# An output projection by seven products of half-size blocks, in two attention layers of a fused network

## The chip, the core and the metric

The kernel runs on one core of a Trainium2 chip. The metric is the device time of one execution in microseconds; the median of three executions is given, and a profile of one execution shows where the time lies. The core's engines are named TensorE (PE), VectorE (DVE), ScalarE (ACT), GpSimd (POOL) and SyncE (SP); SyncE issues the transfers spoken of here.

## The reference

Four layers work on x of shape 2 x 512 x 32 x 32 (batches, channels, pixels). Layer 0 is a deformable attention with an MLP, layer 1 a linear attention. Layers 2 and 3, the ones that matter, are both a self-attention with eight heads of 64 channels over 1024 pixels; they differ in the number of groups of the normalisation:

```python
xn  = group_norm(x)                                  # 8 groups in layer 2, 32 in layer 3
qkv = einsum('oc,bcn->bon', qkv_w, xn) + qkv_b       # 1536 x 512 weights
q, k, v = heads of qkv
attn = softmax(einsum('bhcn,bhcm->bhnm', q, k) * 64 ** -0.5)
att  = einsum('bhnm,bhcm->bhcn', attn, v)            # 512 channels x 1024 pixels
x    = x + einsum('oc,bcn->bon', proj_w, att) + proj_b
```

The last line is the output projection: a 512 x 512 weight times a 512 x 1024 matrix, for each of two batches. All is computed in float32.

## The kernel before

x stays in SBUF the whole time, as `xs[b][t]`: per batch four tiles of 128 channels by 1024 pixels. `P` is 128, `CT` = 4 the tiles of channels, `HF` = 512 half of the pixels, `DH` = 64, `NB` = 8 blocks of 128 keys.

Layers 2 and 3 go through `attention`, which first makes queries, keys and values (`queries_keys_values`) and then, where a bound on the logits holds (it does for these inputs), runs `heads_bounded`. The other branch, `heads_general`, is built but not executed.

Queries, keys and values are already made by seven products in place of eight. A matrix product of 2 x 2 blocks can be had from seven products of sums of the blocks, in Winograd's form of Strassen's scheme. The table `SEVEN` (line 50) says for P1 to P7 which of seven left operands (the four blocks of the weight and three sums, `left_sums`, L624) meets which of seven right operands. The MLP of layer 0 does the same (L649 its matmuls, L628 to L631 the sums of its weights, L763, L764 and L767 adds to x on GpSimd).

`heads_bounded` has 16 units: batch b, pair of heads p, half of the pixels h. A unit has 8 steps, one per block of 128 keys. In a step TensorE computes scores (L1246, 4 matmuls) into a PSUM tile of the ring `ps_s` (two tiles), ScalarE takes the exponential into an SBUF tile tagged `e` (L1250, pool `ep` of six), and TensorE multiplies it with the values two steps later (L1275). The sum of the exponentials over the keys is shared: GpSimd adds e0+e1, then e3 and e5 (L1255, L1257, tile `some`), VectorE adds e2+e4, e6, e7 and then `some` (L1260, L1262, L1264). L1284 and L1285 add two halves of a unit's output into the tile of its query (`data[b][0][p]`, named q in the profile). `divide`, four steps into the next unit, sums the exponentials over partitions on TensorE (L1292), copies (L1296), adds (L1297), takes the reciprocal (L1298), multiplies (L1300) and adds the bias of the values (L1301).

After the last unit the projection runs: for each batch and each of four tiles of 128 output channels `project_block` issues 8 matmuls (two halves of the pixels by four tiles of input channels) into one tile of `ps_s`, and VectorE evicts the two halves with bias and residual in one instruction each (L607). The last unit's `divide` stands behind the first block. In layer 2 the statistics of layer 3's normalisation for batch 0 (`channel_means`, L1171 and L1172; `group_means`, L1178 to L1189; `norm_first`) are issued behind blocks 1 to 6; in layer 3 each half is stored to the output as soon as it is evicted (L609). The projection's weights are loaded at the start of `heads_bounded` (L947, four transfers of 256 KB per layer).

TensorE's order is the order of the code (`manual_schedule`); the order on the other engines in `heads_bounded` is decided by a scheduler, which also gives free buffers of a tag to the next tile that asks. [...] Where two engines touch the same PSUM bank, the framework puts them one after the other.

Of the kernel before, what the change touches and what calls it, by code (L numbers as in the profile page):

```python
# [11 lines left out]
F32 = mybir.dt.float32  # L12
AF = mybir.ActivationFunctionType
ALU = mybir.AluOpType
# [4 lines left out]
P = 128  # L19
B, C, H, W = 2, 512, 32, 32  # L20
N = H * W
CT = C // P
NB = N // P
HF = 512
# [25 lines left out]
SEVEN = {"P1": (0, 0), "P2": (1, 2), "P3": (6, 3), "P4": (3, 6), "P5": (2, 4), "P6": (4, 5), "P7": (5, 1)}  # L50


class Net:
# [539 lines left out]
    def project_block(self, acc, att, w, bias: str, b: int, o: int, out):  # L593

        nc = self.nc
        for h in range(2):
            for t in range(CT):
                nc.tensor.matmul(  # L598
                    acc[:, h, :],
                    lhsT=w[t][:, o * P : (o + 1) * P],  # L600
                    rhs=att[t][:, h * HF : (h + 1) * HF],
                    start=(t == 0),
                    stop=(t == CT - 1),
                )
        for h in range(2):
            xt = self.xs[b][o][:, h * HF : (h + 1) * HF]
            nc.vector.scalar_tensor_tensor(xt, acc[:, h, :], self.col(bias, o), xt, ALU.add, ALU.add)  # L607
            if out is not None:
                nc.sync.dma_start(out[b, o][:, h * HF : (h + 1) * HF], xt)  # L609
# [330 lines left out]
            self.nc.sync.dma_start(got[-1], src)  # L940
        return got

    def projection_weights(self, pool, k: int):
        got = []
        for t in range(CT):
            got.append(pool.tile([P, C], F32, tag=f"proj{t}", name=f"proj{k}{t}"))
            self.nc.sync.dma_start(got[-1], self.io[f"l{k}_proj"][t])  # L947
        return got

    def averages(self):  # L950
        self.avg, self.means = {}, {}
        for k in (2, 3):
            self.avg[k] = self.norm.tile([P, P], F32, tag="avg", name=f"avg{k}")
            self.nc.sync.dma_start(self.avg[k], self.io[f"l{k}_avg"])

    def attention(self, k: int, weights, out, meanwhile=lambda: None):


        nc = self.nc
        with ExitStack() as ctx:  # L960
            one = self.pool(ctx, f"a{k}")
            ones = one.tile([P, DH], F32, tag="ones", name=f"ones{k}")
            nc.vector.memset(ones, 1.0)
            data = []
            for b in range(B):
                qs = [one.tile([P, N], F32, tag=f"q{b}{t}", name=f"q{k}{b}{t}") for t in range(CT)]
                ks = [one.tile([P, N], F32, tag=f"k{b}{t}", name=f"k{k}{b}{t}") for t in range(CT)]
                v = [one.tile([P, 2, C], F32, tag=f"v{b}{n}", name=f"v{k}{b}{n}") for n in range(NB // 2)]
                data.append((qs, ks, v))
            small_logits, got = self.queries_keys_values(k, weights, ones, data, meanwhile)  # L970
            if k == 2:
                self.means_tiles(3, 0)
                self.first[3] = self.first_block(3, 0)

            with self.tc.If(small_logits > 0) as cmp:
                self.heads_bounded(k, ones, data, out)
            with cmp.Else():
                self.heads_general(k, data)
                with ExitStack() as ctx2:
                    proj = self.projection_weights(self.pool(ctx2, f"a{k}_w_p"), k)  # L980
                    ps = self.pool(ctx2, f"a{k}_ps_p", 2, psum=True)
                    for b in range(B):
                        for o in range(CT):
                            acc = ps.tile([P, 2, HF], F32, tag="ps", name=f"pbg{k}{b}{o}")
                            self.project_block(acc, data[b][0], proj, f"pb{k}", b, o, out)
                    if k == 2:
                        for t in range(CT):
                            self.channel_means(3, 0, t)
                        for _ in self.group_means(3, 0, ps.tile([P, 2, HF], F32, tag="ps", name="gm3g")):
                            pass  # L990
                        self.norm_first(3)
            return got
# [227 lines left out]
    def heads_bounded(self, k, ones, data, out):  # L1220
# [5 lines left out]
        nc = self.nc  # L1226
        halves = [slice(0, DH), slice(DH, P)]
        with ExitStack() as ctx:
            proj = self.projection_weights(self.pool(ctx, f"b{k}_w"), k)
            ep = self.pool(ctx, f"b{k}_e", 6)  # L1230
            ap = self.pool(ctx, f"b{k}_a", 1)
            ap2 = self.pool(ctx, f"b{k}_a2", 2)
            ps_s = self.pool(ctx, f"b{k}_ps_s", 2, psum=True)
            ps_o = self.pool(ctx, f"b{k}_ps_o", 1, psum=True)
# [52 lines left out]
            def divide(unit):  # L1287
                b, p, h, state = unit
                d = ps_o.tile([P, 2, HF], F32, tag="d", name=f"d{k}{b}{p}{h}")
                for r, rows in enumerate(halves):  # L1290
                    for par in range(2):
                        nc.tensor.matmul(  # L1292
                            d[halves[par], r, :], lhsT=ones[rows, :], rhs=state["sum"][rows, par, :], start=True, stop=True
                        )
                t = ap.tile([P, HF], F32, tag="r", name=f"r{k}{b}{p}{h}")
                nc.scalar.copy(t, d[:, 0, :])  # L1296
                nc.vector.tensor_tensor(t, d[:, 1, :], t, ALU.add)  # L1297
                nc.vector.reciprocal(t, t)  # L1298
                res = data[b][0][p][:, h * HF : (h + 1) * HF]
                nc.vector.tensor_tensor(res, res, t, ALU.mult)  # L1300
                nc.vector.tensor_scalar(res, res, self.col(f"vb{k}", p), None, ALU.add)  # L1301

            units = [(b, p, h, {}) for b in range(B) for p in range(CT) for h in range(2)]
            steps = [(unit, n) for unit in units for n in range(NB)]
            with self.tc.manual_schedule(engines={mybir.EngineType.PE}):


                for i in range(len(steps) + 5):
                    if i < len(steps):
                        score(*steps[i])  # L1310
                    for j in ([], [i - 3, i - 2])[i % NB == 3] if i % NB in (2, 3) else [i - 2]:
                        if 0 <= j < len(steps):
                            value(*steps[j])
                    if i % NB == 4 and NB < i < len(steps):
                        divide(steps[i - NB][0])
                for b in range(B):
                    for o in range(CT):
                        acc = ps_s.tile([P, 2, HF], F32, tag="s", name=f"pb{k}{b}{o}")
                        self.project_block(acc, data[b][0], proj, f"pb{k}", b, o, out)
                        if b == o == 0:  # L1320
                            divide(units[-1])
                        if k == 2:
                            n = b * CT + o
                            if 1 <= n <= CT:
                                self.channel_means(3, 0, n - 1)
                            elif n == CT + 1:
                                steps = self.group_means(3, 0, ps_o.tile([P, 2, HF], F32, tag="d", name="gm3"))
                                next(steps)
                            elif n == CT + 2:
                                next(steps, None)  # L1330
                                self.norm_first(3)

    def heads_general(self, k, data):
        with ExitStack() as ctx:
# [102 lines left out]
def _blocks(w):  # L1437

    return np.ascontiguousarray(w.T).reshape(-1, P, w.shape[0])


def _slabs(w):


    s0, _, s1, m = w.shape
    w = w.reshape(s0, 2, 2, P, s1, 2, m // 2).transpose(0, 4, 3, 5, 1, 2, 6)
    return w.reshape(s0 * s1, P, 4, 2, m // 2)
# [30 lines left out]
def _layout(i):  # L1478
    f = {k: np.asarray(v) for k, v in i.items()}
    a = {k[8:]: v for k, v in f.items() if k.startswith("L0_conv_")}  # L1480
    l1 = {k[8:]: v for k, v in f.items() if k.startswith("L1_conv_")}
    l2 = {k[8:]: v for k, v in f.items() if k.startswith("L2_conv_")}
    l3 = {k[8:]: v for k, v in f.items() if k.startswith("L3_conv_")}
# [5 lines left out]
    def over(v):  # L1489
# [33 lines left out]
        "l1_b": np.concatenate([l1["bv"], l1["bq"], l1["bk"]]),  # L1523
        "l2_qk": _slabs(l2["qkv_w"][: 2 * C].T.reshape(1, C, 1, 2 * C))[0],
        "l2_v": _slabs(l2["qkv_w"][2 * C :].T.reshape(1, C, 1, C))[0],
        "l2_proj": _blocks(l2["proj_w"]),
        "l2_avg": _average(C // 8),
        "l3_qk": _slabs(w3[: 2 * C].T.reshape(1, C, 1, 2 * C))[0],
        "l3_v": _slabs(w3[2 * C :].T.reshape(1, C, 1, C))[0],
        "l3_proj": _blocks(l3["w_proj"]),  # L1530
        "l3_avg": _average(C // 32),
    }

# [15 lines left out]
```

## Time and profile before

The time before is 3453.8 us (median of 3 runs, 3453.35 to 3453.96). The profiled execution has a span of 3450.1 us, with a mean granted TensorE clock of 0.997. Busy microseconds of each engine in the stretches of layers 2 and 3, by start and end in the span:

| Stretch | us | PE | DVE | ACT | POOL |
|---|---|---|---|---|---|
| heads of layer 2, 2702.4 to 2942.7 | 240.3 | 236.3 | 164.7 | 146.3 | 113.6 |
| projection of layer 2, to 3001.1 | 58.4 | 56.9 | 27.2 | 4.0 | 9.7 |
| queries, keys, values of layer 3, to 3149.5 | 148.4 | 147.5 | 89.9 | 25.1 | 53.1 |
| heads of layer 3, to 3389.1 | 239.6 | 236.1 | 164.4 | 145.0 | 113.4 |
| projection of layer 3 and end, to 3450.1 | 61.0 | 56.4 | 20.0 | 1.2 | 0.0 |

In a row of the timeline the first number is the start in us from the beginning of the span, the second the time from there to the end of what was merged into the row; then engine, line of the code, operation, written and read tiles, shape and count. What stands in brackets is idle time of that engine just before, and what ended it. A float32 matmul shows as two records, so 64 matmuls of a projection are 128 records. PEld is the load of weights into the array and SPq the issue of a transfer by SyncE.

### The profile page before, as it was taken

What the parts mean: (1) busy time and instruction counts of PE and PEld (TensorE: products, weight loads), DVE (VectorE), ACT (ScalarE), POOL (GpSimd) and SP (SyncE); (2) the same over time, 40 slices, a digit from 0 to 9 for tenths busy, and PEclk for the clock granted to TensorE, in tenths of its full rate; (3) what the DMA queues carried; (4) which work ended last, traced back from release to release, by engine and by line L of the source; (5) the groups of instructions that cost most, each with busy time, mean ns of one, the idle gap of its engine ahead of it and who ended that gap; (6) DMA issues with size and microseconds to landing.
All of it is one profiled execution on the core that took longest, in us unless ns stands there. A gap on an engine that the chain in (4) does not pass through costs nothing.

```text
span 3450.1 us, 60119 instructions
## 1 busy us (share of the span) xinstructions
PE 3394.9 (98%) x25280; PEld 1260.6 (37%) x25280; DVE 2313.2 (67%) x2539; ACT 2017.4 (58%) x2100; POOL 2078.3 (60%) x1584
## 2 busy tenths in 40 slices
PE   7999999999999999999999999999999999999999
PEld 2333333333333333333333334444555433455333
DVE  6877777777767567777776764575556577555774
ACT  5877877887787577877887761111111466113661
POOL 4778777787787577787788874442323444234441
PEclk9999999999999999999999999999989999999999
DMA  6878777877887577887888872111000100000001
GB/s 154 156 144 159 149 155 146 156 158 141 157 161 141 108 156 149 155 157 144 167 168 158 159 152 76 49 37 37 1 1 0 50 1 2 1 0 13 2 1 50
DMA packets 103247, 342.64 MB, mean 99 GB/s; under 512 B 12720, under 2 KB 14384, under 8 KB 100144
## 3 DMA queue, kind: packets, MB, share of 16 engines
q0 software_dynamic: 73296, 266.90, 41.0%
q1 hardware_dynamic: 28656, 69.68, 6.8%
q8 instruction: 202, 3.31, 0.4%
q10 hardware_dynamic: 1008, 2.06, 0.2%
q14 instruction: 85, 0.70, 0.1%
HBM read 67.27 MB, written 4.46 MB: 21 GB/s over the span
## 4 chain that ended last, share of the span: by engine, by line
PE 80%; DVE 15%; ACT 2%; POOL 1%; issue 1%; DMA 0%; DVEq 0%; ACTq 0%; SPq 0%; POOLq 0%
PE hp L486 46%; DVE h L455 3%; PE pb L598 3%; DVE r L1298 3%; PE sim L518 3%; PE o L1275 2%; DVE sum L1262 2%; PE s L1246 2%; PE qk20P L1041 1%; PE qk30P L1041 1%; PE m_0P L649 1%; PE qk21P L1041 1%; PE m_5P L649 1%; PE m_4P L649 1%; PE m_2P L649 1%; PE qk31P L1041 1%
## 5 line engine op out<-in xcount | busy, mean ns | idle before, releaser
L486 PE MATMUL hp<-h,w 128*32 128x512 f32 x16384 | 1831.1, 593 | 5.5 <-DVE h L455 3.6
L455 DVE CUSTOM_DVE_ANT_1 h<-tx,bank 128x1024 f32<-128x1024 f32 x1024 | 1180.4, 1215 | 332.9 <-PE hp L486 310.6
L491 ACT ACTIVATE h<-hp,magb 128x1024 f32<-128x1024 f32 x1024 | 1122.0, 1111 | 416.7 <-PE hp L486 415.6
L486 PEld LDWEIGHTS hp<-h,w 128*32 128x32 f32 x16384 | 543.1, 110 | 1216.1 <-issue 1120.9
L478 POOL DMA_DIRECT2D h<-h x509 | 451.7, 1023 | 392.5 <-ACT h L497 334.0
L504 POOL TENSOR_TENSOR h<-h,h 128x1024 f32<-128x1024 f32 x255 | 613.5, 2406 | 21.3
L502 POOL TENSOR_SCALAR h<-h,flip 128x1024 f32<-128x1024 f32 x256 | 447.7, 1749 | 0.9 <-ACT h L491 0.9
L1250 ACT ACTIVATE e<-s 128x1024 f32<-128x1024 f32 x256 | 258.2, 1024 | 177.6 <-PE s L1246 164.1
L493 ACT ACTIVATE h<-h,flip 128x1024 f32<-128x1024 f32 x256 | 291.3, 1138 | 0.0
L1275 PE MATMUL o<-e,v 64*64 64x512 f32 x2048 | 261.0, 592 | 6.7 <-DVE q L1285 6.7
L1246 PE MATMUL s<-q,k 64*64 64x512 f32 x2048 | 259.8, 589 | 2.6 <-DVE v L1079 1.8
L1257 POOL TENSOR_TENSOR some<-some,e 128x1024 f32<-128x1024 f32 x64 | 151.5, 2367 | 75.7 <-ACT e L1250 73.3
L495 POOL TENSOR_SCALAR h<-h,flip 128x1024 f32<-128x1024 f32 x128 | 144.9, 1132 | 77.4 <-ACT h L491 76.0
L1255 POOL TENSOR_TENSOR some<-e,e 128x1024 f32<-128x1024 f32 x32 | 75.5, 2361 | 190.8 <-DVE sum L1264 155.6
L497 ACT ACTIVATE h<-h,flip 128x1024 f32<-128x1024 f32 x128 | 145.6, 1137 | 0.0
L518 PE MATMUL sim<-h,ends 128*32 128x512 f32 x1024 | 141.0, 592 | 0.0
L1260 DVE TENSOR_TENSOR sum<-e,e 128x1024 f32<-128x1024 f32 x32 | 46.4, 1451 | 136.1 <-ACT e L1250 136.1
L1275 PEld LDWEIGHTS o<-e,v 64*64 64x64 f32 x2048 | 75.8, 133 | 157.3 <-issue 123.7
L1246 PEld LDWEIGHTS s<-q,k 64*64 64x64 f32 x2048 | 78.7, 133 | 143.4 <-issue 117.9
L628 POOL TENSOR_TENSOR mlp_w<-mlp_w 128x512 f32<-128x512 f32 x16 | 22.4, 1401 | 161.0 <-DMA mlp_w<-in_mlp_w 136.7
L708 ACT ACTIVATE mh<-mh,cols 128x512 f32<-128x512 f32 x64 | 46.2, 722 | 124.2 <-DVE mh L726 65.5
L1029 POOL TENSOR_TENSOR sq<-q 128x512 f32<-128x512 f32 x32 | 33.3, 1039 | 139.7 <-DVE q L1048 95.6
(456 smaller groups left out, 3280.2 us busy)
## 6 DMA issues: line engine op xcount, KB each, us to landing
h<-h POOLq DMA_DIRECT2D x509, 512.0 KB, 6.5
lb<-logs SPq DMA_DIRECT2D x63, 512.0 KB, 5.2
mlp_w<-in_mlp_w SPq DMA_DIRECT2D x16, 1024.0 KB, 4.9
x<-in_x SPq DMA_DIRECT2D x8, 512.0 KB, 9.7
qkw<-in_l_qk SPq DMA_DIRECT2D x2, 2048.0 KB, 8.3
out<-x SPq DMA_DIRECT2D x16, 256.0 KB, 2.1
vw<-in_l_v SPq DMA_DIRECT2D x2, 1024.0 KB, 7.4
proj<-in_l_proj SPq DMA_DIRECT2D x8, 256.0 KB, 5.1
```

What stands on the lines that cost most here:

```text
L455: self.nc.vector._custom_dve(TENSOR_ADD_SAT, out=h[:, k, :, :], in0=x[:, jj, 2 * r + k, :].unsqueeze(1).to_broadcast([P, H, W]), in1=y[:, ...
L478: nc.gpsimd.dma_start(to, what, accum_op=ALU.add)
L486: nc.tensor.matmul(hp[rows, cut], lhsT=self.l0w2[:, 32 * q : 32 * q + 32], rhs=h1[k][:, cut], start=True, stop=True)
L491: nc.scalar.activation(y, hp, AF.Relu, bias=self.magb[:, q : q + 1])
L493: nc.scalar.activation(ys[0], ys[0], AF.Copy, scale=self.flip[:, 0:1])
L502: nc.gpsimd.tensor_scalar(y, y, self.flip[:, 2:3], 1.0, ALU.mult, ALU.mult)
L504: (nc.vector if final else nc.gpsimd).tensor_tensor(y, y, ys[2], ALU.add)
L518: nc.tensor.matmul(sims[u][at : at + 32, :], lhsT=self.ends[:, 28 - 4 * o : 60 - 4 * o], rhs=z[jj][:, h * HF : (h + 1) * HF], start=(o == ...
L1246: nc.tensor.matmul(s[halves[c], par, :], lhsT=ks[p][rows, at : at + DH], rhs=qs[p][rows, cut], start=True, stop=True)
L1250: nc.scalar.activation(e, s, AF.Exp, scale=DH**-0.5)
L1257: nc.gpsimd.tensor_tensor(state["some"], state["some"], e, ALU.add)
L1275: nc.tensor.matmul(o[halves[par], r, :], lhsT=v[n // 2][rows, n % 2, at : at + DH], rhs=e[rows, par, :], start=(n == 0), stop=(n == NB - 1),)
```

## The change

In layers 2 and 3 the projection, too, is done by seven products of halves in place of eight: the weight's 512 x 512 is cut into four blocks of 256 x 256, and the attention's 512 x 1024 into four of 256 x 512. A product is 4 matmuls (two tiles of output channels by two of input channels), and a batch takes 7 products.

It is for fewer matmuls on TensorE. In return there are sums:

- of the weights (`project_left`): four of 128 x 512 on GpSimd per layer, written in the code after step 72 of 128. The weights are one transfer of 1 MB in a layout of blocks.
- of the attention (`project_right`): eight of 128 x 512 per batch, all on GpSimd in batch 0, half of them on VectorE in batch 1. Their four tiles of 128 x 1024 are taken from the ring of the exponentials, tag `e`, which goes from six tiles to five, since the weights and their three sums need more room.
- of the products (`project`): ScalarE copies P1 into a tile `u`; VectorE adds products to x or to `u`; GpSimd adds `u` to x where more than one block of the output needs it.

The last unit's `divide` now stands behind P1 of batch 0, and the statistics of layer 3 for batch 0 behind P1, P3, P6 and P7 of batch 1, as x of batch 0 is complete only after P4.

In the order in which the changed program is built, the four weight sums come first on GpSimd in each `heads_bounded`, ahead of e0+e1 of the first unit. On VectorE the first batch reads: the last unit's sums, a sum for batch 1, L1285, evictions of P1, L1297, the reciprocal, evictions of P3 alternating with L1300 and L1301, evictions of P2.

```diff
-            proj = self.projection_weights(self.pool(ctx, f"b{k}_w"), k)
-            ep = self.pool(ctx, f"b{k}_e", 6)
+            wp = self.pool(ctx, f"b{k}_w", 1)
+            ep = self.pool(ctx, f"b{k}_e", 5)
...
+            def project_left():
+                w = wp.tile([P, 7, 2, 2 * P], F32, tag="proj", name=f"proj{k}")
+                nc.sync.dma_start(w[:, 0:4], self.io[f"l{k}_proj"])
+                self.left_sums(nc.gpsimd, w[:, 0:4], w[:, 4:7])
+                return [w[:, i] for i in range(7)]
+
+            def project_right(b):
+                att = data[b][0]
+                r = [[att[2 * (i // 2) + c][:, (i % 2) * HF : (i % 2 + 1) * HF] for c in range(2)] for i in range(4)]
+                t = [ep.tile([P, 2, HF], F32, tag="e", name=f"pt{k}{b}{i}") for i in range(4)]
+                t1, t2, t3, t4 = ([x[:, c, :] for c in range(2)] for x in t)
+                for c in range(2):
+                    eng = nc.vector if b == 1 and c == 0 else nc.gpsimd
+                    eng.tensor_tensor(t1[c], r[1][c], r[0][c], ALU.subtract)
+                    eng.tensor_tensor(t2[c], r[3][c], t1[c], ALU.subtract)
+                    eng.tensor_tensor(t3[c], r[3][c], r[1][c], ALU.subtract)
+                    eng.tensor_tensor(t4[c], r[2][c], t2[c], ALU.subtract)
+                return [r[0], t3, r[2], r[3], t1, t2, t4]
...
+                for which in ("P1", "P3", "P2", "P6", "P7", "P5", "P4"):
+                    a, ri = SEVEN[which]
...
+                    acc = ps_s.tile([P, 2, HF], F32, tag="s", name=f"pb{k}{b}{which}")
+                    for p in range(2):
+                        for c in range(2):
+                            nc.tensor.matmul(acc[:, p, :], lhsT=left[a][:, c, p * P : (p + 1) * P],
+                                             rhs=right[ri][c], start=c == 0, stop=c == 1)
+                    for p in range(2):
+                        got = acc[:, p, :]
+                        u = us[:, p, :]
+                        if which == "P1":
+                            nc.scalar.copy(u, got)
+                            add(vec, p, 0, got, True)
+                        elif which == "P3":
+                            add(vec, p, 1, got, True)
+                        elif which == "P2":
+                            add(vec, p, 0, got)
+                            store(p, 0)
+                        elif which == "P6":
+                            vec.tensor_tensor(u, got, u, ALU.add)
+                        elif which == "P7":
+                            u3 = u3s[:, p, :]
+                            vec.tensor_tensor(u3, got, u, ALU.add)
+                            add(pool, p, 3, u3)
+                            add(pool, p, 2, u3)
+                        elif which == "P5":
+                            vec.tensor_tensor(u, got, u, ALU.add)
+                            add(pool, p, 1, u)
+                            store(p, 1)
+                            add(vec, p, 3, got, True)
+                            store(p, 3)
+                        else:
+                            add(vec, p, 2, got, True)
+                            store(p, 2)
+                    yield
...
-                for b in range(B):
-                    for o in range(CT):
-                        acc = ps_s.tile([P, 2, HF], F32, tag="s", name=f"pb{k}{b}{o}")
-                        self.project_block(acc, data[b][0], proj, f"pb{k}", b, o, out)
-                        if b == o == 0:
-                            divide(units[-1])
...
+                    if i == len(steps) // 2 + NB:
+                        left = project_left()
+                right = project_right(0)
+                for n, _ in enumerate(project(0, left, right)):
+                    if n == 0:
+                        divide(units[-1])
+                    elif n == 1:
+                        right = project_right(1)
+                for n, _ in enumerate(project(1, left, right)):
+                    if k == 2:
+                        if n < 2:
+                            self.channel_means(3, 0, 2 * n)
+                            self.channel_means(3, 0, 2 * n + 1)
+                        elif n == 3:
+                            means = self.group_means(3, 0, ps_o.tile([P, 2, HF], F32, tag="d", name="gm3"))
+                            next(means)
+                        elif n == 4:
+                            next(means, None)
+                            self.norm_first(3)
```

The calls `add` and `store` add to the block i of x with or without the bias, and store it where the layer is the last.

## Prediction

> **What bounds the kernel now.** I read the page first: engine shares, then the chain that ended last.
>
> ```profile
> PE 3394.9 (98%) x25280; PEld 1260.6 (37%) x25280; DVE 2313.2 (67%) x2539; ACT 2017.4 (58%) x2100; POOL 2078.3 (60%) x1584
> ...
> PE 80%; DVE 15%; ACT 2%; POOL 1%; issue 1%; DMA 0%; DVEq 0%; ACTq 0%; SPq 0%; POOLq 0%
> ```
>
> TensorE is busy 98% of the span and carries the chain, so a matmul less is time gained unless TensorE waits instead. Next, the timeline of the end of layer 3's heads and the first projection blocks:
>
> ```profile
> 3386.40 2.75 PE L1275 MATMUL o<-e,v 64*64 64x512 f32 x24
> ...
> 3389.09 7.13 PE L598 MATMUL pb<-q,proj 128*128 128x512 f32 x16
> ...
> 3390.95 1.23 DVE L1264 TENSOR_TENSOR sum<-sum,some 128x1024 f32<-128x1024 f32 x1
> ...
> 3398.65 3.35 DVE L1298 RECIPROCAL r<-r 128x512 f32<-128x512 f32 x1
> ...
> 3411.21 1.41 DVE L607 SCALAR_TENSOR_TENSOR x<-pb,cols,x 128x512 f32<-128x512 f32 x2 [5.46 <-PE pb L598]
> ```
>
> A block of 8 matmuls (16 records) is 7.13 us, less the 0.27 by which a last record overhangs: 6.86, or 0.858 us a matmul. TensorE does not pause; VectorE idles 5.46 of every 6.87 us; GpSimd does nothing. This is the room that the change fills. Third, the start of the heads of layer 3, where the timeline shows what the weight sums can hold up:
>
> ```profile
> 3149.54 3.23 SPq L947 DMA_DIRECT2D proj<-in_l_proj  x4
> ...
> 3152.91 2.36 POOL L1255 TENSOR_TENSOR some<-e,e 128x1024 f32<-128x1024 f32 x1 [12.52 <-ACT e L1250]
> ...
> 3157.50 1.02 ACT L1250 ACTIVATE e<-s 128x1024 f32<-128x1024 f32 x1 [0.69 <-PE s L1246]
> ...
> 3159.81 1.07 PE L1246 MATMUL s<-q,k 64*64 64x512 f32 x8
> ```
>
> The rows are the load of the projection's weights, GpSimd's first sum (e0+e1), exponential number 5 (counted from 0) and score 7. Last, the same kind of load and sums in layer 0:
>
> ```profile
> 2185.64 0.33 SPq L672 DMA_DIRECT2D mlp_w<-in_mlp_w  x1
> 2190.63 1.27 POOL L628 TENSOR_TENSOR mlp_w<-mlp_w 128x512 f32<-128x512 f32 x1 [5.47 <-DMA mlp_w<-in_mlp_w]
> 2191.98 1.27 POOL L629 TENSOR_TENSOR mlp_w<-mlp_w 128x512 f32<-128x512 f32 x1
> ```
>
> From issue of 1 MB to the first sum: 5.0 us; then one sum each 1.345 us.
>
> [...] L1260, two SBUF inputs beside GpSimd's sums, takes 1.45 us in the mean, where L1264 takes 1.23. [...] no row of before has both read one bank. [...] here 1.27 against 0.69 us for 128x512 (L1081, L1285).
>
> **The change, part by part.**
>
> *Matmuls.* Per layer 64 become 2 x 7 x 4 = 56: 8 x 0.858 = 6.86 us less, 13.7 in both.
>
> *Weight sums.* The four sums are written after step 72, but the scheduler puts them first on GpSimd, ahead of e0+e1, in both layers. Queued behind them are all sums "some" of the first unit. With five exponential buffers, exponential 5 needs the buffer of e0 or e1, so it waits for e0+e1; score 7 needs the PSUM tile that exponential 5 reads; TensorE stands at score 7. Layer 3: load issued 3149.54, + 5.0 = 3154.54; four sums to 3159.85; e0+e1 to 3162.3 (2.36); exponential 5 to 3163.4; score 7 at 3163.4 instead of 3159.81: 3.6 us. Layer 2, where the load is issued at 2702.91 and score 7 starts at 2713.82: 2707.9, 2713.2, 2715.7, 2716.7, so 3.0 us. Sum 6.6. Later units catch up nothing, since TensorE is full.
>
> *Five buffers elsewhere.* In a steady unit (3373 to 3388) exponential 7 starts at 3386.7 and needs e2, whose last reader (L1260) ends at 3383.1; exponential 5 starts at 3383.2 and needs e0, read until 3379.6. The margins are over 3 us: nothing.
>
> *Sums of the attention for the first batch.* Eight on GpSimd, 10.2 us, beginning when its last "some" ends, 2.3 us before the projection. The first is needed by P6, 11.15 us into the projection: ready at about 2.8. Nothing.
>
> *VectorE's queue in the first batch.* P6 needs the PSUM tile of P3, whose second eviction stands behind this row, counted from the projection's start: sums until 3.1; a sum for the second batch 0.69; L1285 0.68; P1's evictions, which alternate with ScalarE's copies of the same banks (0.75, 0.58, 0.75), until 6.8; L1297 0.69; reciprocal 3.35, until 10.9; P3's first half 0.75, L1300 0.69, second half 0.75: 13.04. TensorE is ready at 11.15: 1.95 us, in each layer.
>
> *Border of the batches.* P1 of batch 1 waits for P5's evictions (four VectorE instructions of 0.69 to 0.75 behind one more sum): 0.4 us in each layer. In layer 2 the statistics of batch 0, until now spread behind blocks with 5.46 us of room each, queue up here: the eviction of P4 stands behind a statistic that waits for GpSimd's last adds to x (6 x 1.27 plus a sum after P7), which costs P3 0.86 us; the evictions of P1 stand behind six more statistics of 0.67, which costs P2 2.03.
>
> So layer 3's projection gains 6.86 - 2.35 = 4.5, layer 2's 6.86 - 5.24 = 1.6.
>
> *Contention.* Three sums for batch 1 are released on VectorE and GpSimd by the same matmul, both reading two SBUF inputs. At no cost 0; at the 1.8 and 0.95 us that such pairs show in layer 0 (L628 up to 1.79, L638 0.952), carried through the same queue, 1.7 us for both layers; at 2.25 and 1.2 (the slowest adds of L764 and L763 there) 3.4. I take 1.
>
> *End.* After P7 of batch 1 GpSimd does six adds of 1.27: it ends about 1.7 us after the last matmul, as VectorE does, but the last store of x now stands in SyncE's order behind three others that wait for those adds, about 0.35 each (L672): 1.1 us. At the border to layer 3, evictions end 0.1 later; GpSimd's query-key weight sums (four of 2.4) move from 2957 to behind its adds, ready some 11.5 us after the projection, while the first product that needs them, the third, starts at 1.55 (the gap before L1041) + 2 x 6.86 = 15.3: nothing.
>
> Sum: -13.7 + 6.6 + 2.35 + 5.24 + 1.2 + 1.0 = +2.7 us.
>
> **Rivals.** (a) *The queues are looser than I count*: reciprocal and evictions interleave so that P6 and the border cost nothing. Then -13.7 + 6.6 + 1.2 = -6, 3448. If GpSimd's late first sum also cost nothing, 3441: the gain in full. For it: VectorE is under half busy in the projection on average (27.15 of 58.40 us in layer 2). Against: its queue is in order and the row of work at the start is fixed. (b) *Slower*: the loads land after 7.4 us, as vw of the attention layers does in the page's issues (+4.8 for both), and contention takes 3.4: +10, 3464. For it: all the terms sit on TensorE. Against: the load is alone on its queue, as in layer 0.
>
> **How the numbers follow.** Forecast (losses about equal the saving, within 0.2%, 6.9 us): 0.80; rival (a), in full, faster: 0.06; rival (b), or a wait that I don't see, slower: 0.14. Predicted: 3453.8 + 2.7 = 3456.5. Low: rival (a)'s first form, 3448.5; high: contention 3.4 and loads at 6 us (+2.4 +2), 3461.5.
>
> **What would show it.** Right: score 7 of each layer's first unit 3 to 3.6 us late, released by ScalarE, GpSimd's e0+e1 behind L628 to L631; TensorE idle before P6 about 2 us with the reciprocal on VectorE; layer 2's P3 and P2 of batch 1 waiting on VectorE; the two projections near 57 and 52 us. Wrong: exponential 5 on time, or no gap in the projections (then 3441 to 3448), or a wait in each unit of the heads (then far over 3461).

## The result and the profile after

The changed kernel takes 3473.1 us in the median (3472.9 to 3474.2, 4 runs) where the kernel before takes 3453.9 (3453.4 to 3456.6): the ratio is 1.0055, with a 95% interval of 1.0037 to 1.0072. It is slower by 19 us; the prediction was 3456.5, and its range ended at 3461.5.

The page of the changed kernel, first its busy times, then the chain that ended last:

```profile
PE 3391.0 (98%) x25248; PEld 1256.5 (36%) x25248; DVE 2361.7 (68%) x2579; ACT 2022.5 (58%) x2108; POOL 2162.1 (62%) x1640
...
PE 77%; DVE 17%; ACT 2%; POOL 2%; issue 1%; DMA 1%; DVEq 0%; SPq 0%; POOLq 0%; ACTq 0%
```

TensorE has 32 matmul records fewer and 3.9 us less busy time, not the 13.7 us that 16 matmuls of 0.858 us should take away: what remains must be running slower somewhere. VectorE has gained 48 us of busy time with only 40 instructions more, which at some 0.7 us each are 28, so others have become longer; its share of the chain went from 15% to 17%. Next, what TensorE waited for in layers 2 and 3 (us in total, times, longest):

```profile
PE s L1240 <- ACT e L1244: 10.9, 3, 6.0
PE d L1286 <- DVE sum L1258: 7.8, 2, 3.9
PE pb21P L1345 <- DVE x L1326: 2.1, 3, 0.9
PE pb31P L1345 <- DVE x L1326: 0.6, 1, 0.6
PE pb20P L1345 <- DVE x L1326: 0.4, 1, 0.4
```

The first row is the wait of score 7 that was forecast, and larger (0.8 us of it stood in the kernel before too). The second was not forecast at all: `d` is the product of the last unit's divisor (L1286), and it waits for VectorE's last addition of exponentials. The waits at P6 (pb20P) and at the border of the batches (pb21P, pb31P) were forecast, and are smaller. The timeline of the start of the heads of layer 2:

```profile
2704.19 0.33 SPq L1301 DMA_DIRECT2D proj<-in_l_proj  x1
2711.79 1.27 POOL L628 TENSOR_TENSOR proj<-proj 128x512 f32<-128x512 f32 x1 [17.21 <-DMA proj<-in_l_proj]
2713.14 2.13 POOL L629 TENSOR_TENSOR proj<-proj 128x512 f32<-128x512 f32 x1
2717.91 2.34 POOL L1249 TENSOR_TENSOR some<-e,e 128x1024 f32<-128x1024 f32 x1
2720.28 1.94 ACT L1244 ACTIVATE e<-s 128x1024 f32<-128x1024 f32 x2 [8.17 <-POOL some L1249]
2721.36 1.99 PE L1240 MATMUL s<-q,k 64*64 64x512 f32 x8 [6.05 <-ACT e L1244]
```

The chain is the forecast one: the load, four sums (two are shown), e0+e1, exponential 5, score 7. But the load took 7.6 us from issue to the first sum, where 5.0 had been taken. And the last row holds a surprise: 8 records take 1.99 us, where 8 such records took 1.07 in the row shown of before. The timeline of the start of the projection of layer 2 in the changed kernel:

```profile
2952.01 3.70 PE L1345 MATMUL pb20P<-q,proj 128*128 128x512 f32 x8
2952.61 3.65 POOL L1314 TENSOR_TENSOR pt<-q,pt 128x512 f32<-128x512 f32 x2
2952.85 4.49 DVE L1256 TENSOR_TENSOR sum<-sum,e 128x1024 f32<-128x1024 f32 x2
2957.45 2.10 DVE L1258 TENSOR_TENSOR sum<-sum,some 128x1024 f32<-128x1024 f32 x1
2959.60 1.47 PE L1286 MATMUL d<-sum,ones 64*64 64x512 f32 x8 [3.88 <-DVE sum L1258]
2961.00 8.40 PE L1345 MATMUL pb20P<-q,proj 128*128 128x512 f32 x16
2969.84 2.38 PE L1345 MATMUL pb20P<-pt,proj 128*128 128x512 f32 x5 [0.44 <-DVE x L1326]
```

VectorE's two additions of e take 4.49 us, where before they took 2.55 (2941.93); the last one takes 2.10, where it took 1.23. GpSimd adds attention tiles at the same time, two in 3.65 us, where one alone takes 1.27. So the divisor's product stands for 3.88 us, and the 16 records behind it take 8.40 in place of 7.13. Last, the windows view of the first 3 us after the wait at score 7 and of the next 3. A row gives the stretch and its length, the busy us (and instructions) of PE, PEld, DVE, ACT and POOL, then the granted TensorE clock, the DMA share and GB/s:

```profile
2721.30:2724.30 3.00, 2.94 (x16) 1.05 (x20) 1.50 (x1) 1.78 (x3) 2.92 (x2) 0.50 0.01 3
2724.30:2727.30 3.00, 3.00 (x28) 0.86 (x24) 2.70 (x2) 1.18 (x2) 1.66 (x1) 0.94 0.00 0
```

After the wait TensorE gets half its clock for some 3 us. Finer windows give the bounds of all such stretches in layers 2 and 3: 2717.8 to 2724.6 (it began while TensorE still stood at score 7), 2960.2 to 2963.6, 3175.2 to 3178.6 and 3414.1 to 3417.6, each behind one of the four long waits. TensorE had work for 3.3, 3.4, 2.8 and 3.4 us of them, and half of that is lost: 1.6, 1.7, 1.4 and 1.7 us, 6.4 in all.

By stretch, before and after: the heads of layer 2 take 240.3 and 248.3 us, the projection of layer 2 58.4 and 60.9, queries, keys and values of layer 3 148.4 both times, the heads of layer 3 239.6 and 244.9, the projection of layer 3 with the end 61.0 and 64.9. That is +8.0, +2.5, 0, +5.3 and +3.9; the remaining 1.3 of the 21.0 us between the two spans lies ahead of layer 2, where nothing was changed.

Theories for the runs. **First:** the four weight sums hold up score 7. **Second:** GpSimd's additions exclude VectorE's, so that the divisor comes late. **Third:** after such a wait TensorE runs at half clock. Rivals: five buffers of exponentials cost time in every unit; VectorE's queue is late on its own; the order of TensorE's products is what matters.

### The profile page after: what moved, and what is told of

It reads as the page before. It is cut to its first block, busy times and chain, and to the rows that moved or that the text cites. A ratio compares the mean times of both kernels' runs of the same rounds, so it can differ in the third digit from the quotient of the medians.

```text
span 3471.1 us, 60176 instructions
## 1 busy us (share of the span) xinstructions
PE 3391.0 (98%) x25248; PEld 1256.5 (36%) x25248; DVE 2361.7 (68%) x2579; ACT 2022.5 (58%) x2108; POOL 2162.1 (62%) x1640
## 3 DMA queue, kind: packets, MB, share of 16 engines
q10 hardware_dynamic: 1008, 2.06, 0.2%
## 4 chain that ended last, share of the span: by engine, by line
PE 77%; DVE 17%; ACT 2%; POOL 2%; issue 1%; DMA 1%; DVEq 0%; SPq 0%; POOLq 0%; ACTq 0%
PE hp L486 46%; DVE r L1292 3%; DVE h L455 3%; PE sim L518 3%; DVE sum L1256 2%; PE o L1269 2%; PE qk20P L1035 1%; PE qk30P L1035 1%; PE m_0P L649 1%; PE m_6P L649 1%; PE m_4P L649 1%; PE m_3P L649 1%; PE m_1P L649 1%; PE qk31P L1035 1%; PE qk21P L1035 1%; PE m_5P L649 1%
## 5 line engine op out<-in xcount | busy, mean ns | idle before, releaser
L1244 ACT ACTIVATE e<-s 128x1024 f32<-128x1024 f32 x256 | 258.2, 1024 | 190.8 <-PE s L1240 176.5
L1240 PE MATMUL s<-q,k 64*64 64x512 f32 x2048 | 261.6, 593 | 12.7 <-ACT e L1244 10.9
L1269 PE MATMUL o<-e,v 64*64 64x512 f32 x2048 | 262.2, 595 | 6.4 <-DVE q L1279 6.4
L1269 PEld LDWEIGHTS o<-e,v 64*64 64x64 f32 x2048 | 75.9, 133 | 158.6 <-issue 125.4
L628 POOL TENSOR_TENSOR mlp_w<-mlp_w 128x512 f32<-128x512 f32 x16 | 22.6, 1415 | 160.6 <-DMA mlp_w<-in_mlp_w 130.7
L1292 DVE RECIPROCAL r<-r 128x512 f32<-128x512 f32 x32 | 107.3, 3353 | 1.1
```

Of the source, the lines that this page charges most:

```text
L1240: nc.tensor.matmul(s[halves[c], par, :], lhsT=ks[p][rows, at : at + DH], rhs=qs[p][rows, cut], start=True, stop=True)
L1244: nc.scalar.activation(e, s, AF.Exp, scale=DH**-0.5)
L1269: nc.tensor.matmul(o[halves[par], r, :], lhsT=v[n // 2][rows, n % 2, at : at + DH], rhs=e[rows, par, :], start=(n == 0), stop=(n == NB - 1),)
```

## Experiments on the first wait

**Five buffers alone.** The kernel before with one number changed.

```diff
-            ep = self.pool(ctx, f"b{k}_e", 6)
+            ep = self.pool(ctx, f"b{k}_e", 5)
```

> The kernel before with five buffers of the exponentials in place of six, nothing else. Theory (the weight sums on GpSimd, not the buffer count, hold up the first unit): 3454 us, no difference, no wait of score 7 in either layer, heads 240 us each. Rival (five buffers cost time by themselves, all through the heads): the 13.3 us by which the two heads grew, so about 3467.

Measured: 3454.1 us against 3453.9, ratio 1.0002 (0.9993 to 1.0010). The rival of five buffers falls; that step of the prediction ("nothing") held.

**The weight sums with eight products.** The eight products of the kernel before, with five buffers. The weights come in one load of 1 MB, and four sums are added, which go to spare tiles.

```diff
+                w = wp.tile([P, 7, 2, 2 * P], F32, tag="proj", name=f"proj{k}")
+                nc.sync.dma_start(w[:, 0:4], self.io[f"l{k}_proj"])
+                nc.gpsimd.tensor_tensor(w[:, 5], w[:, 0], w[:, 2], ALU.subtract)
+                nc.gpsimd.tensor_tensor(w[:, 4], w[:, 2], w[:, 3], ALU.add)
+                nc.gpsimd.tensor_tensor(w[:, 5], w[:, 4], w[:, 0], ALU.subtract)
+                nc.gpsimd.tensor_tensor(w[:, 6], w[:, 1], w[:, 5], ALU.subtract)
```

> The eight products of the kernel before, with five buffers, the weights loaded as one piece of 1 MB and four sums of weights on GpSimd, written where the change writes them; the sums go to tiles that no product reads. Theory (the sums stand first on GpSimd and hold up score 7): TensorE waits 6.0 us in layer 2 and 4.0 in layer 3 and then runs 1.6 and 1.4 us slower at half clock: 3454 + 13 = 3467. Rival (the heads lose their time to something that the seven products do): 3454. Rival (five buffers alone): what the kernel with only five buffers takes.

Measured: 3467.9 us, ratio 1.0041 (1.0027 to 1.0055), 14.0 more than before where 13 were expected. TensorE waits 5.4 and 5.3 us at score 7 here, and the clock behind both waits is 0.50. So four sums of 1.3 us, off the path by their count, cost 14 us by where they stand.

**The weight sums later.** GpSimd's order is written out in the heads, so that the sums stand where the source has them, in the ninth unit.

```diff
-            with self.tc.manual_schedule(engines={mybir.EngineType.PE}):
+            with self.tc.manual_schedule(engines={mybir.EngineType.Pool, mybir.EngineType.PE}):
                 for i in range(len(steps) + 5):
...
+            with self.tc.manual_schedule(engines={mybir.EngineType.PE}):
                 right = project_right(0)
```

> The changed kernel with GpSimd's order written out in the heads too, so that the four sums of weights stand where the source has them, in the ninth unit, and not ahead of the first sum of exponentials. Theory: the wait before score 7 and the half clock after it go in both layers, 6.0 + 1.6 + 4.0 + 1.4 = 13 us: 3460. Rival (the same work costs the same wherever it stands): 3473. Rival (four sums in a row delay the first sum of the ninth unit, which then holds its score 7): 3463 to 3466.

Measured: 3471.2 us (3468.1 to 3471.9), ratio 1.0049 (1.0035 to 1.0062): only 2 us came back, and the main expectation of 3460 failed. The wait at score 7 is gone (0.9 us is left, as before). A new one stands in the ninth unit of each layer, here that of layer 2:

```profile
2839.47 4.50 DVE L1256 TENSOR_TENSOR sum<-sum,e 128x1024 f32<-128x1024 f32 x2
2840.75 2.13 POOL L631 TENSOR_TENSOR proj<-proj 128x512 f32<-128x512 f32 x1
2845.95 1.95 PE L1269 MATMUL o<-e,v 64*64 64x512 f32 x16 [3.84 <-DVE q L1279]
```

It is the picture of the start of the projection: VectorE's two additions take 4.50 us beside GpSimd's, so the output of the unit before is evicted late (L1279), and its PSUM tile is free late. The last rival in the expectation named a late e0+e1 at score 7, for 3 to 6 us. The path is another, and the cost larger: 3.84 and 3.85 us of waiting, and half clock behind the second. The second theory reaches further than the projection.

## Experiments on the second wait

**Without the attention's sums.** The products of batch 0 read the attention itself where the sums would stand; the rest is kept.

```diff
-                right = project_right(0)
+                att = data[0][0]
+                r = [[att[2 * (i // 2) + c][:, (i % 2) * HF : (i % 2 + 1) * HF] for c in range(2)] for i in range(4)]
+                right = r + r[:3]
```

> The changed kernel without the eight sums of the attention for batch 0 (they are left out: its seven products read the attention itself in their place), all else kept. Theory (GpSimd's sums slow VectorE's sums of exponentials, so that the last divisor comes late): VectorE's two additions and the last one go back to about 2.5 and 1.2 us, the wait of 3.9 us before the divisor's product and the 1.7 us of half clock after it go in each layer, P6's wait grows from 0.4 to the 1.95 us that was forecast: 2 x (5.6 - 1.5) = 8 us less, 3465. Rival (VectorE's own queue, with the evictions, is late by itself): the wait stays, 3473.

Measured: 3465.7 us (3464.2 to 3467.5), ratio 1.0034 (1.0021 to 1.0046), 7.4 less than the changed kernel where 8 were expected. Its timeline at the start of the projection of layer 2:

```profile
2952.43 1.22 DVE L1256 TENSOR_TENSOR sum<-sum,e 128x1024 f32<-128x1024 f32 x1
...
2956.70 1.22 DVE L1258 TENSOR_TENSOR sum<-sum,some 128x1024 f32<-128x1024 f32 x1
...
2957.97 1.09 PE L1286 MATMUL d<-sum,ones 64*64 64x512 f32 x8 [1.78 <-DVE sum L1258]
```

With GpSimd idle, VectorE's additions are back at 1.22 us each. A wait of 1.78 us stays, since the scheduler now puts four sums for batch 1 (0.68 us each) between them; the clock after it is 1.00. P6 waits 0.9 us in each layer, half of what had been forecast.

**The divisor later.** Only the place in TensorE's order changes.

```diff
-                    if n == 0:
+                    if n == 2:
                         divide(units[-1])
-                    elif n == 1:
+                    elif n == 4:
                         right = project_right(1)
```

> The changed kernel with the last unit's divisor two products later, behind P2 of batch 0 (and the sums of the attention for batch 1 behind P7), so that TensorE doesn't stand at it; GpSimd's sums beside VectorE's stay. Theory (what costs is that TensorE waits for a VectorE slowed by GpSimd): VectorE's additions stay at 4.5 and 2.1 us, P1's evictions end about 9.7 us into the projection, P2 waits about 2.8 us for them, [...] in place of 3.9 + 1.7 in each layer: 2 x 2.8 = 6 us less, 3467. Rival (the slow additions hold up the same work whatever the order): 3473. Rival (the reciprocal, now between P2's evictions and P6's, becomes a new wait of up to 3 us in each layer): 3473 to 3476.

Measured: 3479.0 us, ratio 1.0069 (1.0055 to 1.0083), 5.9 more than the changed kernel, not 6 less:

```profile
2965.56 5.71 PE L1345 MATMUL pb20P<-q,proj 128*128 128x512 f32 x8 [4.77 <-DVE x L1326]
```

P2 needs the PSUM tile of P1, whose evictions stand behind the same slow additions on VectorE; the wait forecast at 2.8 us is 4.77. The first rival, that the slow additions hold up whatever comes next, is what the trace shows, though its 3473 was too low. The new wait is longer than the old one because one more sum for batch 1 (1.74 us) and evictions that alternate between VectorE and ScalarE stand behind the additions.

## Experiments on what excludes what

**The sums spread over the heads.** All four weight sums, the eight for batch 0 and three for batch 1 stand singly behind GpSimd's first sum of a unit, the attention's in the dead tiles of the keys.

```diff
+                    if i % NB == 1 and i < len(steps):
+                        if 1 <= i // NB <= 4:
+                            left_step(i // NB - 1)
+                        elif i // NB in between:
+                            right_sum(*between[i // NB])
```

> The changed kernel with its sums put one by one between GpSimd's sums of exponentials: the four of the weights in units 1 to 4, the eight of the attention of batch 0 in units 5 to 12, three of batch 1 in units 13 to 15, those of the attention written to the tiles of the keys, which no one needs by then. Theory: score 7 and the divisor wait for nothing, the heads take 240 us as before; what is left is what was forecast for VectorE's queue, 1.95 us at P6 in each layer, 0.5 and 2.5 at the border of the batches, and the longer end of 3.65: -13.7 + 3.9 + 3.0 + 3.65 = -3, 3451. Rival (each sum delays VectorE's additions by contention, and so the eviction of o, wherever it stands: 0.5 us in most units): 3460 or more.

Measured: 3480.6 us, ratio 1.0075 (1.0061 to 1.0088); the rival was right in kind, and its 0.5 us in most units too low. The waits at score 7 and almost all of those at the divisor are gone, but the matmuls with the values (L1269) wait 37.5 us for the eviction of o, in 28 units, where they wait 6.4 in the changed kernel: 1.1 us more in each. VectorE's first addition of a unit, by form, in the heads of layer 2:

```profile
L1254 DVE TENSOR_TENSOR sum<-e,e 128x1024 f32<-128x1024 f32 x15 | 36.9, 2460 | 64.6 <-ACT e L1244 64.6
```

It takes 2460 ns where it took 1458 before (L1260 there): the added sum moves GpSimd's next one wholly on top of it.

**The same with the divisor later.** The edit of the kernel with the late divisor on top of this.

> As the kernel with the sums spread over the heads, and the last unit's divisor behind P2 of batch 0. Theory: the reciprocal no longer stands ahead of P3's second eviction, P6 does not wait, 3.9 us less: 3447. Rival (the reciprocal now holds up P6's evictions and so P5): 3451.

Measured: 3481.0 us, ratio 1.0075 (1.0062 to 1.0089), no gain. The wait of 1.0 us at the divisor goes, but those at the first products of layer 2's batch 1 grow from 1.0 to 3.8 us.

**Another place, and a fill in place of the sums.** First the sums behind GpSimd's last sum of a unit; then, in the same place, a fill with a constant, somewhat shorter (0.96 us, a sum 1.27), which reads no tile.

```diff
-                    if i % NB == 1 and i < len(steps):
+                    if i % NB == 6 and i < len(steps):
...
-                nc.gpsimd.tensor_tensor(to, x, y, op)
+                nc.gpsimd.memset(wide[:, 4 + n // 2 : 6 + n // 2], 0.5)
...
+                if eng is nc.gpsimd and in_heads:
+                    eng.memset(data[b][1][what - 1], 0.5)
+                    return
```

> As the kernel with the sums spread over the heads, but each behind GpSimd's last sum of exponentials of a unit, where GpSimd is idle for over 5 us, in place of behind its first. Theory (VectorE's and GpSimd's sums of two SBUF tiles exclude one another, and a unit has no room left: three of 2.36 us on GpSimd, four of 1.22 and one of 0.69 on VectorE are 12.7 of 13.7 us, so a 1.27 us sum costs about 1 us wherever it stands): VectorE's chain to the eviction of o is late by about 1 us in each of the 30 units with a sum, 3475 to 3481. Rival (only the place was bad: the sum pushed GpSimd's second sum onto VectorE's first): heads of 240 us, 3451 to 3455.

> The same, with the sums in the heads left out: in each one's place GpSimd fills 128x1024 of the same tile with a constant, which reads nothing. Theory (it is the reading that excludes): VectorE's additions stay at 1.22 to 1.43 us, the waits for the eviction of o stay at 6 us in all, heads of 240 us, 3451 to 3455. Rival (any work of GpSimd, or its writes, slows VectorE's additions): 3470 or more.

Measured: with sums 3469.9 us, ratio 1.0049 (1.0033 to 1.0064); with fills 3448.6, ratio 0.9986 (0.9979 to 0.9993). In the heads of layer 2, the multiplication of `divide` (two SBUF inputs) with sums beside it:

```profile
L1294 DVE TENSOR_TENSOR q<-q,r 128x512 f32<-128x512 f32 x14 | 20.3, 1452 | 0.5
```

and with fills beside it, with the fills themselves:

```profile
L1294 DVE TENSOR_TENSOR q<-q,r 128x512 f32<-128x512 f32 x15 | 10.4, 692 | 0.5
...
L1312 POOL MEMSET k<- 128x1024 f32 x11 | 10.5, 959 | 0.0
```

1452 ns against 692: a sum of GpSimd kept VectorE's instruction off for 0.76 us, a fill did not. That gave 0.8 us in 28 units (waits for o of 29.3 us, against 8.1 with fills), less than the 1 us in 30 units expected, because the sum meets a short instruction here and ends before VectorE's next one. So it is the reading of SBUF tiles that excludes here, not GpSimd's being busy: a fill kept it busy for 0.96 us, and the multiplication took 692 ns, as in the kernel before (691, L1300). VectorE was held for about as long as GpSimd's sum still ran: in layer 2 of the late weight sums the multiplication (2836.68, 1.46 us) began 0.90 us before the end of a sum (L628, 2836.30, 1.28 us), and took 0.77 us longer than 0.69. This explains why spreading could not help. A unit of 13.7 us holds three such sums on GpSimd (2.36 us each) and on VectorE four of 1.22 and one of 0.69: 12.7 us for what takes turns where it meets. That no place in a unit is free is argued from this sum; two places were tried.

**Half as many weight sums.** The eight products again, with the last two of the four sums removed.

```diff
-                nc.gpsimd.tensor_tensor(w[:, 5], w[:, 4], w[:, 0], ALU.subtract)
-                nc.gpsimd.tensor_tensor(w[:, 6], w[:, 1], w[:, 5], ALU.subtract)
```

> The eight products with five buffers, the load of 1 MB, and only the first two of the four sums of weights on GpSimd (no product reads them). Two sums are 2.7 us less, so score 7 waits 2.7 us in each layer in place of 5.4 and 5.3. Theory [...]: full clock after both waits, 3454 + 5.4 = 3459. Rival (any wait of microseconds costs the half clock): 3462. The granted clock in the 4 us after the wait tells them apart more surely than the time: 1.00 or 0.50.

Measured: 3463.5 us (3461.1 to 3465.4), ratio 1.0025 (1.0016 to 1.0034), nearer the rival's 3462 than 3459. The wait in layer 2, then the clock from 1 us behind it:

```profile
2719.32 1.92 PE L1240 MATMUL s<-q,k 64*64 64x512 f32 x8 [2.97 <-ACT e L1244]
```

```profile
2720.30:2722.30 2.00, 2.00 (x16) 0.64 (x12) 1.41 (x1) 1.02 (x1) 1.92 (x2) 0.50 0.00 0
```

Waits of 2.97 and, in layer 3, of 2.54 us cost the half clock too (0.50 behind both); the theory, full clock after both waits, falls. In the kernel with the late weight sums the other case stands: of two equal waits, that of 3.84 us in layer 2 was followed by a clock of 1.00, that of 3.85 in layer 3 by 0.50.

The traces show what went with it. The stretches at half clock in layers 2 and 3, up to the last products, are one or two times 3.413 us long, and within a run they begin on a fixed grid: in the changed kernel at 2717.83, 2960.17, 3175.21 and 3414.14 us, which are 71, 63 and 70 times 3.413 us apart. Cut into intervals on each run's own grid, the traces show how long TensorE stood in each. First three intervals of the late weight sums around the wait of 3.84 us, then two of the spread sums around a wait of only 2.03 us in layer 3:

```profile
2840.61:2844.02 3.41, 1.50 (x16) 0.30 (x8) 3.25 (x2) 2.48 (x4) 2.19 (x2) 1.00 0.00 0
2844.02:2847.43 3.41, 1.48 (x16) 0.65 (x20) 1.82 (x2) 0.00 (x0) 1.99 (x1) 1.00 0.00 0
2847.43:2850.84 3.41, 3.41 (x40) 1.19 (x34) 0.94 (x1) 1.32 (x2) 2.72 (x2) 1.00 0.00 0
...
3404.48:3407.89 3.41, 1.38 (x16) 0.36 (x12) 3.31 (x4) 1.72 (x2) 1.35 (x1) 1.00 0.00 0
3407.89:3411.30 3.41, 3.41 (x20) 1.07 (x16) 1.55 (x1) 0.00 (x0) 3.41 (x3) 0.50 0.02 5
```

The wait of 3.84 us falls on two intervals with 1.9 us of idle in each, and no half clock follows. The wait of 3.85 us fills one interval, and half clock follows. The wait of 2.03 us lies in one interval, and half clock follows; one of 2.04 us in layer 2 of the same run, of which 1.75 lie in one interval, has none. Over all fourteen traces, from 2640 to 3436 us, each of the 22 intervals with 2.03 us or more of idle was followed by one at half clock. Of those with less that began at full clock only one was, with 1.91 us; two that began at half clock, with 1.65 and 1.76 us, were followed by another. So the idle time within one interval went with the half clock of the next, not the length of the wait, and 2.03 of 3.41 us were enough here in all 22 cases. Why it is so, the traces do not show.

## A version that beats both

If the reading is what is short in the heads, sums belong where GpSimd has none of its own: into the projection, behind the first blocks. Batch 0 keeps its eight products, and while they run GpSimd makes the sums of the weights and of batch 1, which takes seven.

```diff
+                order = (2, 3, 0, 1)
+                for n, o in enumerate(order):
+                    acc = ps_s.tile([P, 2, HF], F32, tag="s", name=f"pb{k}0{o}")
+                    self.project_block(acc, data[0][0], w, f"pb{k}", 0, o, out)
+                    if n == 0:
+                        divide(units[-1])
+                    elif n == 1:
+                        self.left_sums(nc.gpsimd, w[:, 0:4], w[:, 4:7])
+                        left = [w[:, i] for i in range(7)]
+                        right = project_right(1)
+                    if k == 2 and n:
+                        self.channel_means(3, 0, order[n - 1], order[0])
+                for n, _ in enumerate(project(1, left, right)):
```

> Eight products for batch 0 and seven for batch 1, with five buffers, in both layers: the blocks of batch 0 in the order 2, 3, 0, 1, so that the sums of the weights, all on GpSimd in an order written out, can follow the second block; the sums of the attention of batch 1, all on GpSimd, follow them. Nothing is added to the heads, and one sum (of the weights) runs beside VectorE's at the start of the projection. Theory: half of the saving, 6.9 us, less 0.3 at the border to layer 3 and 3.65 at the end of the kernel: 3451. Rival (the sums still make VectorE late at the last divisor or at the first products of batch 1): 3454 or more.

The second version changes the end of layer 3 in addition.

```diff
-                            add(pool, p, 1, u)
+                            add(vec if k == 3 else pool, p, 1, u)
...
-                        nc.sync.dma_start(out[b, o][:, cut], self.xs[b][o][:, cut])
+                        (nc.sync, nc.scalar)[p].dma_start(out[b, o][:, cut], self.xs[b][o][:, cut])
```

> As the kernel with seven products for batch 1 alone, and at the end of layer 3 the additions of P5 to x on VectorE in place of GpSimd, and every second store from ScalarE's queue. Theory (the end is longer because six stores of 256 KB are released within 3 us and leave one queue one after the other): of the 3.65 us about 2 come back, 3449. Rival (the end is set by the stores' transfer, not by their order): 3451, as without this.

Measured: 3450.7 us, ratio 0.9993 (0.9985 to 1.0001), which is not surely faster; and 3448.9 us, ratio 0.9986 (0.9979 to 0.9992), which is, by 4.6 us or 0.13%. All that TensorE waits for in layers 2 and 3 of the second version:

```profile
PE o L1269 <- DVE q L1279: 6.4, 28, 0.2
PE s L1240 <- DVE v L1073: 1.8, 2, 0.9
PE qk30P L1035 <- DVE x L1323: 1.7, 1, 1.7
PE s L1240 <- ACT e L1244: 0.8, 1, 0.8
```

It is the list of the kernel before, within 0.3 us a row. The heads of layer 2 take 240.4 us, the projection of layer 2 55.1 in place of 58.4. From the last matmul to the end it is 8.3 us in the first version and 7.1 in the second, 4.6 in the kernel before; of the 2 us expected there, the profiles show 1.2, and the medians of the two versions differ by 1.8. Both edits of the end were made at once, so which of them helped stays open.

## Why the prediction was wrong

**The step that failed** is "Sums of the attention for the first batch", costed as "Eight on GpSimd, 10.2 us", "Nothing". Only the question when the sums are ready was asked of it, and there the answer was right. What they do to VectorE meanwhile was not. The last additions of exponentials, "sums until 3.1" in the prediction, ended 7.5 us after the projection's start. The cost is 3.9 us of waiting in each layer and 1.7 of half clock behind it, 11 us in all; the run without these sums shows 7.4, with a wait of 1.8 us left. The trace's figure for it had been quoted ("L1260 ... takes 1.45 us in the mean, where L1264 takes 1.23"), but was applied only to the three sums for batch 1 that one matmul releases on both engines, as contention of 0 to 3.4 us.

**The half clock** is a term that the sum did not have. It took 6.4 us in four places, two of them behind the waits that were foreseen.

**The weight sums** were foreseen by mechanism and place, and mis-sized: 3.0 us in layer 2 were 6.05, 3.6 in layer 3 were 4.0. Rival (b) named the reason for most of it, "the loads land after 7.4 us": in layer 2 the load was issued 1.3 us behind that of vw, 1 MB as well and on the same queue, and took 7.6. So the argument against ("the load is alone on its queue") did not hold there. In the runs with this load, it landed after 6.7 to 7.4 us in layer 2, and after 4.7 to 6.2 in layer 3, where no load of vw stands just ahead of it; that vw is the cause was not tested. The second sum took 2.13 us in place of 1.27, beside VectorE's.

**P6** waited 0.44 us in each layer, not 1.95 (the prediction's own 13.04 less 11.15 is 1.89). The wait ahead of it may have given VectorE time, but with that wait smaller or gone, in the runs without the sums, with spread sums or with fills, P6 waits 0.4 to 0.9; so 1.95 was too much by itself. VectorE did work the row in the order forecast (2952.85 to 2969.69 in layer 2), with P1's evictions and ScalarE's second copy in turn (0.73, 0.59, 0.75 us). The prediction's remark that "no row of before has both read one bank", said of ScalarE and VectorE, is not right either: in layer 0 a copy (L753, 2115.2) and an addition (L742, 2119.2) read the same halves of a PSUM tile in turn.

**The border of the batches** took 2.06 us in layer 2 and 0.56 in layer 3, for 3.29 and 0.4. **The end** took 3.65 us more, for 1.1. The stores show part of the reason, by their time from issue to landing in the changed kernel:

```profile
DMA to landing us min/median/max: 2.1/2.6/4.0
```

In the kernel before the median is 2.1 and the longest 2.6. Six stores of 256 KB are now issued within some 3 us of each other; not only do their issues queue, as the prediction counted, but they also land later. That they hold each other up is argued, not shown.

Summed over both layers, forecast and found: matmuls -13.7 and -13.7; score 7 6.6 and 10.05; divisor 0 and 7.8; half clock 0 and 6.4; P6 3.9 and 0.9; border of the batches 3.7 and 2.6; border to layer 3 and end 1.2 and 3.9; contention of batch 1 1.0, and what there was of it lies within the border's waits. In each of ten pauses the last record's overhang of about 0.25 us also counts, 2.5. With the 1.3 us ahead of layer 2 this gives 21.8, for the 21.0 between the spans. P6 and the border, 4.1 us too large together, hid a part of the miss by luck.

Five buffers cost nothing, as forecast.

## What to carry to other kernels

Before work goes to an engine that looks idle, add up per period what both VectorE and GpSimd read from two SBUF tiles: where the sum is near the period, as 12.7 of 13.7 us here, an instruction more can be paid almost in full (0.8 to 1.1 us for 1.27 here), and where one engine is on the critical path, the other's free time is not free. Price a wait of TensorE above its length once it comes to some 2 us: where 2.03 us or more of it fell within one interval of 3.413 us, half clock followed here and cost up to 1.7 us more. Look for the stage in which the other engine reads nothing, even if only half of a saving can be had there.

## What the runs showed of the hardware that was not expected

- VectorE's and GpSimd's instructions with two SBUF inputs held each other up for most of their length: VectorE's 128x1024 addition went from 1.22 us to 2.25 and 2.46, its 128x512 multiplication from 0.69 to 1.45, GpSimd's 128x512 addition from 1.27 to 2.13. Beside fills of 0.96 us the multiplication took 0.692.
- A VectorE instruction with one SBUF input was slowed as well: L1295 (tensor_scalar, 128x512) took 1.37 us beside GpSimd's sums, 0.49 without.
- TensorE's half clock came, in layers 2 and 3, in stretches of one or two times 3.413 us, on a grid that was fixed within a run. It followed every interval of the grid in which TensorE stood for 2.03 us or more, so it followed one wait of 2.03 us and not one of 3.84 us, which fell on two intervals.
- A load of 1 MB landed after 6.7 to 7.4 us where it was issued 1.3 us behind another of 1 MB, and after 4.7 to 6.2 us where it was not.
